# A feed-forward layer with per-batch weights: another order of the first loads and of the small steps behind them

## The chip, the cores and the metric

The kernel runs on one core of a Trainium2 chip. The core has TensorE for matrix products, VectorE, ScalarE and GpSimd for elementwise work, SyncE (SP) which issues most transfers, and 16 DMA engines between HBM and its on-chip memory SBUF. TensorE writes to PSUM. The metric is the device time of one execution in microseconds (us); the median of several runs is given.

## The reference

```python
W = weights[condition]                         # (64, 64, 64) out of 16 weights of 64x64
h = einsum('bct,bcd->bdt', x, W)               # per batch; x is (64, 64, 1024)
q = unpack6(qweight)                           # (1024, 1024) integers 0..63
w = (q - zero_point) * weight_scale            # per output row
out = x + einsum('bsk,nk->bsn', h, w) + bias   # (64, 64, 1024)
```

Every batch picks one of 16 small weights by its condition (stage 1). The result is multiplied with a large weight that is stored in 6 bits (stage 2). The input is added at the end. All is float32.

## The kernel before, in words

Two batches make a pair p, which fills the 128 partitions: the first batch lies in partitions LO (0 to 63), the second in HI (64 to 127). There are 32 pairs; two pairs make a group g. A value is multiplied as a high and a low half of 16 bits, so that the products keep the accuracy of float32: `hh` and `hl` are the halves of the result of stage 1, `xa` holds both halves of x, and `tab` those of the small weights. To bring the values into the range of the 16-bit type, they are scaled by a power of two, which is taken from a bound on sums of magnitudes: magnitudes (line 269, or 408 and 410 for the first two pairs), one small product on TensorE that spreads the bound (273 or 418), and a few bit operations on VectorE (`powers`, lines 138 to 142). Stage 2 (line 514) is eight K tiles (kt) of two halves and two banks of 512 columns, 32 products for a pair.

All work is put in order by hand. Each engine executes its instructions in the order in which they are written, and waits with semaphores for the others. The first pairs, 0 and 1, go an early way that needs less preparation. Their stage 1 is done in float32 (`early_stage1`, line 430) with `wbd`, a block diagonal of the two weights of the pair. `wbd` is copied out of the loaded weights `w32` by GpSimd and ScalarE (`early_select`, lines 389 and 391). Pair 0 has its x in two halves. The bound of a pair of this kind is the product of the weights' largest magnitude (`early_weights`, lines 396 and 397) and x's largest or summed magnitude (`early_magnitudes`). `early_rows` (line 413) multiplies them; `early_bounds` (418) spreads them on TensorE; `early_scales` makes the scales of it, which `early_high` and `early_low` (438, 445) use to write `hh` and `hl`. `weights_largest` (line 170) takes the largest magnitude of each of the 16 weights; it serves the scales of `tab`, and stands on VectorE ahead of the steps for pair 0. `unpack` (153, 155) takes the 6-bit fields out of the packed words `qr`.

From pair 2 on, stage 1 (line 490) uses the halves in `xa` and the weights of the pair in `wst`. Group 1 (pairs 2 and 3) has its halves written by `stacked_high` on ScalarE (318) and `stacked_low` on VectorE (326). Each of these is done twice for a pair, for the two halves of the partitions. From group 2 on, the halves are moved by DMA (333 to 339). A loop `window(p)` carries pairs 3 to 31, and the change does not touch it.

The transfers go to two queues. SP issues nearly all, in the order of lines 90 to 104; ScalarE issues `cb`, the conditions, and two small loads into a tile `ahead` that nothing reads. Eight semaphores serve the transfers in turn: a transfer waits at its issue until the one before it on the same semaphore has landed.

The tail of the early part, in which pairs 0 to 3 overlap, is the written order of lines 579 to 707. Line 654 (bounds of pair 3's x) stands ahead of the products of pair 1 with tiles 4 to 6 (line 658).

Of the kernel before, what the change touches and what calls it, by code (L numbers as in the profile page):

```python
# [8 lines left out]
F32 = mybir.dt.float32  # L9
# [3 lines left out]
U16 = mybir.dt.uint16  # L13
AF = mybir.ActivationFunctionType
ALU = mybir.AluOpType
# [4 lines left out]
QUNIT = 2.0**-24  # L20
# [9 lines left out]
def adaln_ffn(ctx: ExitStack, tc: tile.TileContext, x, cond, cw, qw, ws, wz, bias, out):  # L30
    nc = tc.nc
    B, C, T = x.shape
    _, NK, D = cw.shape
    N = qw.shape[2]
    P = 128
    NP = B // 2
    NG = NP // 2
    KT = T // P
# [6 lines left out]
    const = ctx.enter_context(tc.tile_pool(name="const", bufs=1))  # L45
# [15 lines left out]
    def load_pair(p, ts_=slice(0, T)):  # L61
        g, i = divmod(p, 2)
        if g not in xts:
            xts[g] = xp.tile([P, 2, T], F32, name="xt")
        nc.sync.dma_start(xts[g][:, i, ts_], xf[:, p, ts_])  # L65
# [10 lines left out]
    def load_q(w, n=1):  # L76
        nc.sync.dma_start(qr[:, w : w + n, :], qv[:, w // 2, w % 2 : w % 2 + n, :])

    w32 = const.tile([P, NK, D], F32, name="w32")
    cb = const.tile([NK, B], I32, name="cb")  # L80
# [3 lines left out]
    bib = const.tile([P, N], F32, name="bib")  # L84
    nc.scalar.dma_start(cb, cond.partition_broadcast(NK))

    ahead = const.tile([NK, 2, 16], F32, name="ahead")
    nc.scalar.dma_start(ahead[:, 0, :], x[0:4, 0 : C : C // 4, 0:16].rearrange("b c t -> (b c) t"))
    nc.scalar.dma_start(ahead[:, 1, :].bitcast(U16), qw[0, 0 : 2 * P : P // 8, 0:32])
    nc.sync.dma_start(w32[LO], cw[LO])  # L90
    load_pair(0, slice(0, T // 2))
    load_pair(0, slice(T // 2, T))
    load_pair(1)
    load_q(0)
    load_q(1)
    load_q(2, 2)
# [31 lines left out]
    kio = const.tile([NK, 1], F32, name="kio")  # L128
# [36 lines left out]
    hot = const.tile([P, B], BF, name="hot")  # L165
# [3 lines left out]
    def weights_largest():  # L169
        nc.vector.tensor_reduce(wmx[LO, 0:NK], w32[LO], AX.X, ALU.max, apply_absolute_value=True)  # L170
# [18 lines left out]
    def weights_powers():  # L189

        powers(tmp["pw"], tmp["pw"], wdn)

    def weights_scaled():
        nc.gpsimd.tensor_tensor(wsc, w32, wdn.unsqueeze(2).to_broadcast([P, NK, D]), ALU.mult)  # L194
# [6 lines left out]

    def weights_hot():

        nc.vector.tensor_scalar(hot[0:NK, :], cb, kio[:, 0:1], None, ALU.is_equal)

    def weights_own():

# [21 lines left out]
    def conditions_of(p, eng=nc.sync):  # L229
        conditions[p] = [  # L230
            eng.value_load(cb[0:1, 2 * p + j : 2 * p + j + 1], min_val=0, max_val=NK - 1) for j in range(2)
        ]
# [19 lines left out]
    st = {}  # L252
# [18 lines left out]
    def bounds(g, sl=BOTH):  # L271
        pl = ps_s.tile([P, 2], F32, name="pl", tag="s")
        nc.tensor.matmul(pl[:, sl], lhsT=ones, rhs=st[g]["l1"][:, sl], start=True, stop=True)  # L273
        st[g]["pl"] = pl
# [39 lines left out]
    def stacked_high(g, i):  # L314

        s = slice(i, i + 1)
        for j, (h, _) in enumerate(HALVES_OF):
            nc.scalar.activation(
                st[g]["xa"][h, i, j], xts[g][h, i], AF.Copy, scale=st[g]["down"][h, s], accum_out=st[g]["xs"][h, s]
            )  # L320

    def stacked_low(g, i, j):

        h, o = HALVES_OF[j]
        xa = st[g]["xa"]
        nc.vector.scalar_tensor_tensor(
            xa[o, i, j], xts[g][h, i], st[g]["down"][h, i : i + 1], xa[h, i, j], ALU.mult, ALU.subtract
        )
# [52 lines left out]
    updown = const.tile([P, 2, 2, 2], F32, name="updown")  # L381

    def early_select(p, j, eng):

        h = (LO, HI)[j]
        k = eng.value_load(cb[0:1, 2 * p + j : 2 * p + j + 1], min_val=0, max_val=NK - 1)
        to, of_ = wbd[h, p, h], w32[LO, ds(k, 1), :].rearrange("p o d -> p (o d)")
        if eng is nc.scalar:
            eng.copy(to, of_)
        else:  # L390
            eng.tensor_copy(to, of_)

    def early_weights(p):

        wl = const.tile([P, 1], F32, name=f"wl{p}")
        nc.vector.tensor_reduce(wl, wbd[:, p, :], AX.X, ALU.max, apply_absolute_value=True)
        nc.vector.tensor_scalar(wm[:, p, :], half, wl[:, 0:1], None, ALU.mult)
# [5 lines left out]
    def early_magnitudes(p, n, ts_, eng):  # L403

        xm[p, n] = const.tile([P, 1], F32, name=f"xm{p}{n}")
        if eng is nc.scalar:
            junk = ap.tile([P, T], BF, name="junk", bufs=1)
            nc.scalar.activation(junk[:, ts_], xts[0][:, p, ts_], AF.Abs, accum_out=xm[p, n])
        else:
            nc.vector.tensor_reduce(xm[p, n], xts[0][:, p, ts_], AX.X, ALU.max, apply_absolute_value=True)  # L410

    def early_rows(p, n):
        nc.vector.tensor_scalar(pb[:, p, n, :], wm[:, p, :], xm[p, n][:, 0:1], LEAST, ALU.mult, ALU.max)
# [7 lines left out]
    def early_scales(p):  # L421
        powers(tmp["pl"], updown[:, p, 0, :], updown[:, p, 1, :], least=False)

    def early_unscales(p):
        for j, h in enumerate((LO, HI)):
            nc.vector.tensor_scalar(st[0]["u"][h, p : p + 1], updown[h, p, 0, j : j + 1], 0.5 / QUNIT, None, ALU.mult)

    def early_stage1(p, ph, kts=range(KT)):
        for kt in kts:
            nc.tensor.matmul(  # L430
                ph[:, kt % ph.shape[1], :, :], lhsT=xts[0][:, p, ts(kt, P)], rhs=wbd[:, p, :], start=True, stop=True
            )

    def early_high(p, ph, kts):
        if p not in hs_pair:
            hs_pair[p] = [hp.tile([P, KT, P], F16, name="hh"), hp.tile([P, KT, P], F16, name="hl")]
        for j, h in enumerate((LO, HI)):
            nc.scalar.activation(
                hs_pair[p][0][:, kts, h], ph[:, :, j, :], AF.Copy, scale=updown[:, p, 1, j : j + 1]
            )  # L440
# [8 lines left out]
    def early_feature_sums(p):  # L449
        s = slice(p, p + 1)  # L450
        pu = ps_s.tile([P, 1], F32, name="pu", tag="s")
        nc.tensor.matmul(pu, lhsT=wbd[:, p, :], rhs=st[0]["xs"][:, s], start=True, stop=True)  # L452
        nc.vector.tensor_copy(st[0]["hs"][:, s], pu)
# [30 lines left out]
    def stage1(p):  # L484
        g, i = divmod(p, 2)
        ph = ps_o[0].tile([P, KT, 2, D], F32, name="ph")
        for kt in range(KT):
            for j in range(2):
                for a in range(2):
                    nc.tensor.matmul(  # L490
                        ph[:, kt, j, :],
                        lhsT=st[g]["xa"][:, i, j, ts(kt, P)],
                        rhs=wsts[g][:, i, a, j, :],
                        start=(a == 0),
                        stop=(a == 1),
                    )
        return ph.rearrange("p k j d -> p k (j d)")
# [26 lines left out]
    def stage2_tiles(p, kts, ks=range(2)):  # L524
        if p not in pos:
            pos[p] = ps_o[1 + p % 2].tile([P, N], F32, name="po", tag="po")
        products(pos[p], p, kts, ks, BANKS, BANKS)
# [49 lines left out]
    ph0a, ph0b = [ps_e.tile([P, KT // 2, 2, D], F32, name="ph0") for _ in range(2)]  # L577
# [2 lines left out]
    early_select(0, 1, nc.scalar)  # L580
    early_select(1, 0, nc.gpsimd)
    early_select(1, 1, nc.gpsimd)
    for n in range(2, 8):
        conditions_of(n, nc.gpsimd)
    weights_largest()
    early_weights(0)
    early_magnitudes(0, 0, slice(0, T // 2), nc.scalar)
    early_stage1(0, ph0a, range(0, 4))
    early_rows(0, 0)
    early_magnitudes(0, 1, slice(T // 2, 3 * T // 4), nc.vector)  # L590
    early_magnitudes(0, 2, slice(3 * T // 4, T), nc.scalar)
    early_rows(0, 1)
    early_rows(0, 2)
    early_weights(1)
    early_stage1(0, ph0b, range(4, KT))
    early_bounds(0, 3)
    early_scales(0)
    early_high(0, ph0a, LOWER)
    early_high(0, ph0b, UPPER)
    early_stage1(1, ph1)  # L600
    unpack(0)
    unpack(1)
# [5 lines left out]
    early_rows(1, 0)  # L608
    weights_turn()
    weights_diagonal()  # L610
    weights_hot()
    unpack(4, 2)
    stage2_tiles(0, range(0, 2), [1])
    unpack(6, 2)
# [3 lines left out]
    weights_bounds()  # L618
    early_bounds(1, 1)
    early_scales(1)  # L620
    weights_powers()
    weights_scaled()
    weights_own()
# [6 lines left out]
    early.close()  # L630
    ps_o.append(ctx.enter_context(tc.tile_pool(name="ps_b", bufs=1, space=bass.MemoryType.PSUM)))
    stacked_high(1, 0)
    for j in range(2):
        stacked_low(1, 0, j)
    weights_high()
    stage2_tiles(0, range(6, KT))
    early_feature_sums(0)
    early_feature_sums(1)
    magnitudes(1, 1)
    early_zero_points(0)  # L640
    early_unscales(0)
    weights_up()
    weights_low()
    unpacking.close()
# [6 lines left out]

    stage2_tiles(1, range(0, 4), [0])
    stage2_tiles(1, range(0, 4), [1])
    bounds(1, SECOND)
    scales(1, SECOND)
    early_minus(0)
    early_res(0)
    stage2_tiles(1, range(4, 7))
    stacked_high(1, 1)
    stacked_low(1, 1, 0)  # L660
    ph = stage1(2)
    stage1_high(2, ph, LOWER)
    stage1_high(2, ph, UPPER)
# [2 lines left out]
    magnitudes(2, 0)  # L666
    magnitudes(2, 1)
    stage1_low(2, ph)
    stacked_low(1, 1, 1)
    weights_of_batches()  # L670
    unscales(1)
    early_unscales(1)


    sums_high(1)
# [103 lines left out]
    p = NP - 1  # L779
# [67 lines left out]
```

## Time and profile before

| | |
|---|---|
| median of 3 runs | 266.77 us (266.57 to 267.13) |
| the profiled execution, its own time | 267.71 us |
| its span | 265.9 us |
| TensorE busy | 260.1 us (98%) |
| VectorE, ScalarE, GpSimd busy | 202.2, 161.7, 175.1 us |
| DMA moved | 53.34 MB, mean 201 GB/s |
| granted TensorE clock | 1.00 |

The profile shows one execution. Its span runs from the first to the last instruction; the execution's own time is longer by what lies around them. In a row of the timeline the first number is the start and the second the duration, both in us, then engine, line and operation, output and inputs, and in brackets how long the engine had been idle and what ended it. A row may hold several instructions (xN). PEld is TensorE's loading of weights, which overlaps the products. The chain that ended last is followed back from the last instruction, at each step to what released it.

### The profile page before, as it was taken

The page shows a single profiled execution, that of the slowest core. Times are in us where ns is not written, and L with a number is a line of the kernel's source. Part 1 is how long each engine was busy: PE and PEld are TensorE (multiplying, and loading weights), DVE is VectorE, ACT ScalarE, POOL GpSimd, SP SyncE. Part 2 cuts the span into 40 slices and gives each one's busy share as a digit, 9 for nine tenths or more (in the row PEclk, how much of TensorE's full clock was granted, in tenths as well). Part 3 has the DMA queues.
Part 4 walks back from the last instruction along what each step waited for, and adds up shares of the span by engine and source line. Part 5 has one row for each costly group of instructions (what it writes and reads, how often), then busy time and mean ns, then how long its engine had stood idle before and what let it go on. Part 6 is the DMA issues. An engine that isn't in the chain of part 4 may idle for free.

```text
span 265.9 us, 5725 instructions
## 1 busy us (share of the span) xinstructions
PE 260.1 (98%) x2159; PEld 139.9 (53%) x2159; DVE 202.2 (76%) x270; ACT 161.7 (61%) x289; POOL 175.1 (66%) x102
## 2 busy tenths in 40 slices
PE   7999999999999999999999999999999999999994
PEld 6655555555455555455555445555545555545553
DVE  3889999695977959598695968959597794955544
ACT  3799899665866556686555767556586555634100
POOL 4026457969595995959789595986829296595200
PEclk9999999999999999999999999999999999999999
DMA  6996078759649796589767797677976664551203
GB/s 178 327 368 239 2 168 261 217 168 270 199 106 325 195 293 178 168 245 238 260 181 225 240 264 244 156 243 217 291 220 178 218 160 137 163 160 79 83 35 123
DMA packets 31948, 53.34 MB, mean 201 GB/s; under 512 B 15152, under 2 KB 15408, under 8 KB 31920
## 3 DMA queue, kind: packets, MB, share of 16 engines
q1 hardware_dynamic: 31824, 52.96, 65.4%
q8 instruction: 17, 0.28, 0.4%
q14 instruction: 11, 0.09, 0.1%
q10 hardware_dynamic: 96, 0.01, 0.0%
HBM read 19.93 MB, written 16.78 MB: 138 GB/s over the span
## 4 chain that ended last, share of the span: by engine, by line
PE 95%; DMA 2%; SPq 1%; DVE 0%; issue 0%
PE po L514 81%; PE ph L490 11%; PE pe L514 3%; DMA xt<-in_x_dram 2%; PE ph L430 1%; PE pu L361 1%; SPq L65 0%; SPq L90 0%; DVE pe L555 0%; DVE xt L560 0%; PE pu L452 0%; PE pl L273 0%; PE pt L174 0%; PE pb__631 L220 0%; PE pl L418 0%
## 5 line engine op out<-in xcount | busy, mean ns | idle before, releaser
L514 PE MATMUL po<-q,hl 128*128 128x512 f16 x496 | 118.3, 379 | 0.0
L514 PE MATMUL po<-q,hh 128*128 128x512 f16 x496 | 118.3, 379 | 0.0
L550 POOL TENSOR_TENSOR xt<-xt,zt 128x1024 f32<-128x1024 f32 x28 | 79.0, 2839 | 48.4 <-ACT zt L548 48.4
L514 PEld LDWEIGHTS <-hl 128*128 128x128 f16 x520 | 50.6, 98 | 59.6 <-DVE hl L506 0.4
L502 ACT CAST hh<-ph 128x1024 f16<-128x1024 f32 (+1 forms) x31 | 30.4, 983 | 79.1 <-PE ph L490 41.5
L543 POOL TENSOR_TENSOR xt<-xt,bib 128x1024 f32<-128x1024 f32 x32 | 74.5, 2351 | 2.1 <-issue 2.1
L514 PEld LDWEIGHTS <-hh 128*128 128x128 f16 x520 | 48.4, 98 | 51.9
L555 DVE SCALAR_TENSOR_TENSOR po<-po,u,scb 128x1024 f32<-128x1024 f32 x27 | 34.8, 1287 | 49.2 <-PE po L514 49.2
L303 DVE SCALAR_TENSOR_TENSOR lf<-xt,down,hf 128x1024 f16<-128x1024 f32 x28 | 60.1, 2184 | 0.0
L506 DVE TENSOR_TENSOR hl<-ph,hh 128x1024 f16<-128x1024 f32 x30 | 36.5, 1216 | 0.1
L490 PEld LDWEIGHTS <-xa 128*128 128x128 f16 x960 | 32.1, 98 | 7.1
L560 DVE TENSOR_TENSOR xt<-po,xt 128x1024 f32<-128x1024 f32 x27 | 33.1, 1225 | 1.9
L490 PE MATMUL ph<-wst,xa 128*128 128x64 f16 x960 | 32.9, 193 | 0.0
L269 ACT ACTIVATE junk<-xt 128x1024 bf16<-128x1024 f32 x30 | 31.7, 1056 | 1.1 <-DMA xt<-in_x_dram 0.3
L293 ACT ACTIVATE hf<-xt,down 128x1024 f16<-128x1024 f32 x28 | 31.9, 1143 | 0.2 <-DVE down L139 0.2
L548 ACT ACTIVATE zt<-zsc,hs 128x1024 f32<-128x1024 f32 x28 | 30.5, 1138 | 0.0
L354 ACT ACTIVATE xh<-xh,xs 64x1 f16<-64x1 f16 x52 | 12.4, 287 | 0.5
L479 POOL TENSOR_TENSOR xt<-xt,res 128x1024 f32<-128x1024 f32 x4 | 9.5, 2365 | 0.0
L245 POOL COPY wst<-tab 128x128 f16 x12 | 4.9, 458 | 4.8 <-DVE tab L200 4.8
L194 POOL TENSOR_TENSOR wsc<-w,wdn 128x1024 f32<-128x1024 f32 x1 | 1.9, 1903 | 9.3 <-DMA w<-in_L_cond_weights_dram 9.3
L514 PE MATMUL pe<-q,hh 128*128 128x256 f16 (+1 forms) x24 | 6.6, 308 | 0.0
L514 PE MATMUL pe<-q,hl 128*128 128x256 f16 (+1 forms) x24 | 6.5, 308 | 0.0
(90 smaller groups left out, 121.3 us busy)
## 6 DMA issues: line engine op xcount, KB each, us to landing
out_dram<-xt SPq DMA_DIRECT2D x31, 512.0 KB, 3.0
xt<-in_x_dram SPq DMA_DIRECT2D x14, 1024.0 KB, 7.5
xa<-hf SPq DMA_DIRECT2D x24, 256.0 KB, 3.8
xa<-lf SPq DMA_DIRECT2D x24, 256.0 KB, 3.8
xt<-in_x_dram SPq DMA_DIRECT2D x3, 512.0 KB, 8.9
wst<-tab SPq DMA_DIRECT2D x48, 32.0 KB, 3.1
xa<-hf SPq DMA_DIRECT2D x8, 128.0 KB, 2.3
xa<-lf SPq DMA_DIRECT2D x8, 128.0 KB, 2.4
```

The lines of the kernel that those rows point to most:

```text
L269: nc.scalar.activation(junk, xts[g][:, i, :], AF.Abs, accum_out=st[g]["l1"][:, i : i + 1])
L293: nc.scalar.activation(st[g]["hf"][:, i, ts_], xts[g][:, i, ts_], AF.Copy, scale=st[g]["down"][:, i : i + 1], accum_out=st[g]["xs"][:, i : ...
L303: nc.vector.scalar_tensor_tensor(st[g]["lf"][:, i, ts_], xts[g][:, i, ts_], st[g]["down"][:, i : i + 1], st[g]["hf"][:, i, ts_], ALU.mult, ...
L490: nc.tensor.matmul(ph[:, kt, j, :], lhsT=st[g]["xa"][:, i, j, ts(kt, P)], rhs=wsts[g][:, i, a, j, :], start=(a == 0), stop=(a == 1),)
L502: nc.scalar.copy(hs_pair[p][0][:, kts, :], ph[:, kts, :])
L506: nc.vector.tensor_tensor(hl[:, kts, :], ph[:, kts, :], hh[:, kts, :], ALU.subtract)
L514: nc.tensor.matmul(po[:, a], lhsT=hs_pair[p][k][:, kt, :], rhs=qT[:, kt, c], start=(kt == 0 and k == 0), stop=(kt == KT - 1 and k == 1),)
L543: nc.gpsimd.tensor_tensor(xt, xt, bib, ALU.add)
L548: nc.scalar.activation(zt, zsc, AF.Copy, scale=st[g]["hs"][:, i : i + 1])
L550: nc.gpsimd.tensor_tensor(xt, xt, zt, ALU.subtract)
L555: nc.vector.scalar_tensor_tensor(po, po, st[g]["u"][:, i : i + 1], scb[:, cols], ALU.mult, ALU.mult)
L560: nc.vector.tensor_tensor(xts[g][:, i, cols], po, xts[g][:, i, cols], ALU.add)
```

## The change

Loads: the first half of pair 0's x is issued ahead of the weights, the second half behind them. Pair 1's x is issued as two halves. Of the two small loads on ScalarE's queue, the ones from x and from the packed words are gone, and one from the weights is there.

Small steps: `weights_hot` and `early_unscales` run on GpSimd, and stand earlier. The magnitude of the first half of pair 0's x runs on VectorE, ahead of `weights_largest`. The step `early_weights(1)` goes behind pair 0's scales.

Order up to pair 3: the feature sums of pairs 0 and 1 go ahead of pair 2's low halves; the bounds of pair 3's x go behind the products of pair 1 with tile 4; pair 3's second low half follows its first.

On TensorE the list of instructions is the same but for the place of one product, that of line 273 for pair 3. VectorE has three rows of instructions fewer in the listing, GpSimd the steps that left it.

```diff
-    ahead = const.tile([NK, 2, 16], F32, name="ahead")
-    nc.scalar.dma_start(ahead[:, 0, :], x[0:4, 0 : C : C // 4, 0:16].rearrange("b c t -> (b c) t"))
-    nc.scalar.dma_start(ahead[:, 1, :].bitcast(U16), qw[0, 0 : 2 * P : P // 8, 0:32])
+    ahead = const.tile([NK, 16], F32, name="ahead")
+    nc.scalar.dma_start(ahead, cw[0 : C : C // NK, 0, 0:16])
+    load_pair(0, slice(0, T // 2))
     nc.sync.dma_start(w32[LO], cw[LO])
-    load_pair(0, slice(0, T // 2))
     load_pair(0, slice(T // 2, T))
-    load_pair(1)
+    load_pair(1, slice(0, T // 2))
+    load_pair(1, slice(T // 2, T))
     load_q(0)
...
     def weights_hot():
-        nc.vector.tensor_scalar(hot[0:NK, :], cb, kio[:, 0:1], None, ALU.is_equal)
+        nc.gpsimd.tensor_scalar(hot[0:NK, :], cb, kio[:, 0:1], None, ALU.is_equal)
...
     def early_unscales(p):
         for j, h in enumerate((LO, HI)):
-            nc.vector.tensor_scalar(st[0]["u"][h, p : p + 1], updown[h, p, 0, j : j + 1], 0.5 / QUNIT, None, ALU.mult)
+            nc.gpsimd.tensor_scalar(st[0]["u"][h, p : p + 1], updown[h, p, 0, j : j + 1], 0.5 / QUNIT, None, ALU.mult)
...
     early_select(1, 1, nc.gpsimd)
+    weights_hot()
     for n in range(2, 8):
         conditions_of(n, nc.gpsimd)
+    early_magnitudes(0, 0, slice(0, T // 2), nc.vector)
     weights_largest()
+    early_stage1(0, ph0a, range(0, 4))
     early_weights(0)
-    early_magnitudes(0, 0, slice(0, T // 2), nc.scalar)
-    early_stage1(0, ph0a, range(0, 4))
     early_rows(0, 0)
...
-    early_weights(1)
     early_stage1(0, ph0b, range(4, KT))
     early_bounds(0, 3)
     early_scales(0)
+    early_unscales(0)
     early_high(0, ph0a, LOWER)
     early_high(0, ph0b, UPPER)
+    early_weights(1)
     early_stage1(1, ph1)
...
-    weights_hot()
...
     early_scales(1)
+    early_unscales(1)
...
     stacked_high(1, 0)
+    stage2_tiles(0, range(6, KT))
+    early_feature_sums(0)
+    early_feature_sums(1)
     for j in range(2):
         stacked_low(1, 0, j)
     weights_high()
-    stage2_tiles(0, range(6, KT))
-    early_feature_sums(0)
-    early_feature_sums(1)
     magnitudes(1, 1)
     early_zero_points(0)
-    early_unscales(0)
...
     stage2_tiles(1, range(0, 4), [1])
+    stage2_tiles(1, [4])
     bounds(1, SECOND)
     scales(1, SECOND)
     early_minus(0)
     early_res(0)
-    stage2_tiles(1, range(4, 7))
+    stage2_tiles(1, range(5, 7))
     stacked_high(1, 1)
     stacked_low(1, 1, 0)
+    stacked_low(1, 1, 1)
...
     stage1_low(2, ph)
-    stacked_low(1, 1, 1)
     weights_of_batches()
     unscales(1)
-    early_unscales(1)
```

## The prediction

> **What bounds the kernel now.** I read the page's busy times first, then the chain that ended last, then the timeline of the first 30 us with the waits of each engine, and last the landings of single tiles.
>
> ```profile
> PE 260.1 (98%) x2159; PEld 139.9 (53%) x2159; DVE 202.2 (76%) x270; ACT 161.7 (61%) x289; POOL 175.1 (66%) x102
> PE 95%; DMA 2%; SPq 1%; DVE 0%; issue 0%
> ```
>
> TensorE is busy 98% and carries 95% of the chain. So only what moves TensorE's start, or opens or closes a hole in it, can move the time. The chain in order of time shows where the start is decided:
>
> ```profile
> 2.48 5.83 DMA xt<-in_x_dram
> 8.31 0.14 issue
> 8.44 2.02 PE ph L430 x16
> 10.46 0.86 PE po L514 x4
> ...
> 25.73 3.45 PE po L514 x16
> 29.18 0.93 PE ph L490 x32
> ```
>
> Pair 1's x, issued at 2.48, lands at 8.31, and TensorE starts pair 1's first stage at 8.44. From there it never stops for long: 16 products of 512 columns take 3.45, 216 ns each. The waits of the PE rows after 8.44 add up to two holes, 0.11 at 30.0 (before line 361) and 0.09 at 35.4 (hl of pair 3). That is all that a better order can win there: 0.2 us.
>
> Before 8.44, and at the second place that matters, the timeline reads:
>
> ```profile
> 4.54 1.21 DVE L170 TENSOR_REDUCE wmx<-w 64x16 bf16<-64x1024 f32 x1 [1.45 <-DMA w<-in_L_cond_weights_dram]
> 5.67 0.27 DVE L396 TENSOR_REDUCE wl<-wbd 128x1 f32<-128x128 f32 x1
> 5.92 2.30 PE L430 MATMUL ph<-wbd,xt 128*128 128x128 f32 x16 [0.84 <-DMA xt<-in_x_dram]
> 7.04 0.42 DVE L410 TENSOR_REDUCE xm<-xt 128x1 f32<-128x256 f32 x1 [0.24 <-DMA xt<-in_x_dram]
> 7.49 0.38 DVE L413 TENSOR_SCALAR pb<-wm,xm 128x2 bf16<-128x2 f32 x2
> 8.05 0.22 PE L418 MATMUL pl<-pb,all_ones 128*128 128x2 bf16 x3
> 22.38 1.15 ACT L318 ACTIVATE xa<-xt,down 64x1024 f16<-64x1024 f32 x1 [0.53 <-DVE down L139]
> 24.91 1.07 ACT L502 CAST hh<-ph 128x512 f16<-128x512 f32 x2
> 25.54 3.14 PEld L514 LDWEIGHTS <-hh 128*128 128x128 f16 x16
> ```
>
> Landings: the weights at 4.43 (issued at 0.74, 3.7 to landing), the first x half at 5.78 (1.39 plus 4.4), the second at 7.01 (DVE's line 410 and PE's second half both start there). The three bound products (line 418) stand in TensorE's order ahead of pair 1. They end at 8.27, only 0.04 before x of pair 1. So two chains end together at 8.3: the loads, and VectorE's row of small steps behind the weights.
>
> **The Trainium skill.** "DMA: Bandwidth & Descriptors", "Issuing engines are not separate DMA queues": loads issued from SP and ACT run on the same 16 DMA engines and interleave. The trace agrees: the 1 KB load ahead of x takes 3.5 us to land, the 4 KB of cb, which meets nothing, 1.5. The same page's "Latency and other measured facts" says that most of a load's fixed cost of about 2 us is the round trip for the write's receipt. Here the 4 KB of cb take 1.5, and that part is paid in any place of the queue: a place earlier is worth only the data time of the load that is passed. "TensorE: Matmul & The Clock Gate", "Back-to-back issue gap", gives N/2.4 + 2.5 ns, 216 ns at 512 columns: what the chain shows, so nothing is left in the products themselves. "GPSIMD Engine Reference", 3.1, puts about 156 ns of dispatch on an instruction; this trace's small GpSimd steps take 0.11 (memset of 64x1) to 0.23 (copy of 64x64).
>
> **The change part by part.** Times against the profiled execution (span 265.9; own time 267.71, which is 0.94 over the median 266.77; I carry differences over to the median).
>
> *1. Order of the loads.* The weights go from first to second on SP, x's first half from second to first. The slots keep their sizes (256 KB each), so x's first half should land near 4.45 (0.74 plus 3.7). For the weights, W: at best little over the first slot's 4.43, since 16 KB per DMA engine must follow 16 KB, say 4.7; at worst the second slot's 5.8 of before. In that slot 15 of the 16 DMA engines had reported by 5.18 in the trace's semaphore records and one came 0.6 later; I take 5.3.
>
> VectorE's row behind W, by starts in the trace: 0.11 to start line 170; 1.13 to line 396; 0.31 to line 397; 0.27 to the first row (413); 0.26 to line 410; 0.45 to the last rows; 0.38 for both. Sum: rows ready at W + 2.91. (Before: W's line ended at 5.75, and from there x's halves set the pace, rows at 7.87.) Moving the first half's magnitude from ScalarE to VectorE costs about 0.68 there (line 170: 1024 elements in 1.21, 256 in 0.42), from 4.5 to 5.2, ahead of the weights. That is free while W is 5.07 or later, and caps the gain below. The last bound product then follows the rows by about 0.25 (0.07 of wait and 0.17 of product), so pair 1 starts at W + 3.16: with 5.3, at 8.46, +0.02 on 8.44. Break-even is W = 5.28, and each us later is a us lost. TensorE's own work on pair 0 starts at W + 0.35 (wbd is written 0.3 after W): 5.65, before the 5.92 of now, and no cost.
>
> *2. Pair 1's x in halves.* One SP issue more (0.43), and 2 KB packets for 4 KB ones, in the trace's DMA records 84 and 159 ns: 16 x 84 - 8 x 159 = 72 ns per engine. Half one lands by about 7.7, half two at 8.4, needed a microsecond into the stage. Gain: the wait for 8.31 goes, but the rows take its place. The loads behind: qr comes 0.07 later; line 155 for it may slip from 9.00 and 9.67 by 0.2, its first product is at 10.3. Cost 0. SP's waits move with the semaphores: zsb is issued after x's second half (about 7.1 instead of 6.36), pair 3's x about 0.7 later. The DMA engines are full from 6 to 20 us in stretches of 1 us (share 0.96 or more, but for one of 0.87), and zsb lands at 16.3 for a use at 20.71. Cost 0; with empty queues it would be 0.7 on a load with 4 us to spare.
>
> *3. The two small loads ahead.* x and qw are no longer touched ahead; cw is. Unknown: 0 to 0.5 us on x's or q's first packets, less 0.3 for a lighter start. I take 0. q's cover is about 0.5: hl of pair 0 (line 445) would end at 11.0, TensorE loads it at 11.16.
>
> *4. Steps to GpSimd.* hot (0.24) and four unscales (0.31 + 0.30) leave VectorE; GpSimd pays five instructions at 0.11 to 0.25, 0.6 to 1.2. It has nothing to do from 13.3, when its reads of the conditions end in the trace's records, to 15.42, where wsc waits for the second half of the weights; the reads start up to 0.9 later. wsc itself is read 1.4 after its end. Cost 0. line 396 for pair 1 goes behind pair 0's powers: 0.5 that VectorE spends before q at 9.3 instead of 8.3. Cost 0.
>
> *5. Second bounds of group 1 behind a tile.* Line 273 moves behind four products: from 21.12 to 21.98, ends at 22.15. From a bounds product's end to ScalarE's line 318 the first such pass took 0.46 (15.73 to 16.19), so line 318 starts at 22.61 instead of 22.38: +0.23. ScalarE is then solid until hh of pair 2 (24.91, first half 0.54, to 25.45), which TensorE loads at 25.54: a cover of 0.09. So 0.14 to 0.2 of new hole; bounds 0 to 0.25, I take 0.17. Queued behind it are all products of pair 2. The wait before line 361 at 30.0 moves with ScalarE: +0.05.
>
> *6. Low halves.* The sums' copies (0.21) come ahead of two low halves of 1.28 and wait for line 452, 0.3; the unscales that left pay for that. The last low half goes ahead of pair 2's hl: ready at 27.9 instead of 28.96 for a use at 29.0, hl at 29.2 for a use at 30.2. Both hidden. VectorE is 0.1 ahead at 34.2, while TensorE is 0.2 later: the 0.09 hole at 35.4 goes.
>
> Sum: +0.02 + 0.17 + 0.05 - 0.09 = +0.15 us; span 266.1, median 266.9.
>
> **Rivals.** *A, slower:* the weights land as late as the second load did, 5.8. Mechanism: line 170's 1.21 us start late, the rows (line 413) end at 8.71, pair 1 starts at 8.96: +0.52, and with the 0.13 of parts 5 and 6, +0.65: 267.4. It decides from W = 5.68. For it: that slot's measured landing. Against: only one engine was that late.
>
> *B, faster:* both first loads land early, x at 4.0 and the weights at 4.75, and x's second half by 6.7, where 10 of its 16 engines had reported by 5.5. Rows at 7.66, pair 1 at 7.91: -0.53; without the hole of part 5 and with the 0.2 of holes closed, -0.73: 266.0. For it: the late engines are few. Against: q would be the next thing late.
>
> *C, it does nothing:* the rows and x of pair 1 ended 0.04 apart before and do so again, and part 5's cover holds: 266.7.
>
> **Chances.** A 0.30, B 0.25, the forecast 0.30 and C 0.15. The smallest difference that a measurement of this kernel tells from none is about 0.2%, 0.53 us; the forecast and C lie inside, A and B outside. So faster 0.25, same 0.45, slower 0.30. The likeliest case alone spans 266.5 to 267.2; with A and B and the unknown of part 3 (0.5 on top of A's lower end), 266.0 to 267.7 leaves out about 2 in 10.
>
> **What would show it.** Right: line 170 starts near 5.4 and the rows end near 8.2; pair 1's first product at 8.3 to 8.6 waits for the bounds, not for x; ScalarE's first line 318 after 22 at about 22.6 plus the shift, and a hole of 0.1 to 0.2 in TensorE at 25.6; none at 35.4. Wrong: line 170 starts at 4.8 or after 5.8, pair 1 waits for x, or TensorE waits at 10.5 for q. A change of more than 1 us would mean a wait past 36 us, where I see no instruction moved.

## The result and the profile after

| | before | after |
|---|---|---|
| median of 20 runs each, on one chip | 267.14 us (266.57 to 267.69) | 267.63 us (267.40 to 268.16) |
| ratio of after to before | | 1.002, interval 1.0013 to 1.0027 |
| the profiled execution, its own time | 267.71 us | 267.60 us |
| its span | 265.9 us | 265.8 us |

The kernel became 0.49 us slower. The forecast was +0.15 on the median of 266.77 that it started from, rounded to 266.9. In the larger set of runs before itself has 267.14, so it is the differences that are compared here. Remarkable is what the two profiled executions say: after's is 0.11 *faster* than before's. So the pair of profiles can't explain the difference of the medians. The fastest of after's 20 runs, 267.40, is slower than before's median.

The page of after, its busy times and the shares of the chain that ended last:

```profile
PE 260.4 (98%) x2159; PEld 140.2 (53%) x2159; DVE 200.1 (75%) x266; ACT 161.1 (61%) x287; POOL 176.2 (66%) x107
PE 94%; DMA 2%; ACT 1%; DVE 1%; issue 1%; SPq 0%; DVEq 0%
```

TensorE still carries nearly all. New are the shares of ScalarE and VectorE, which the chain of after, in order of time, places:

```profile
1.19 4.09 DMA w<-in_L_cond_weights_dram
...
5.39 0.28 DVE wmx L170
...
7.67 0.24 DVE pb L413
...
8.25 1.96 PE ph L430 x16
...
22.36 1.25 ACT xa L318 x2
...
24.89 0.59 ACT hh L502
...
25.54 3.63 PE po L514 x16
```

Before's chain began with x of pair 1. Now it begins with the weights, which land at 5.28, and goes through VectorE's row of small steps to pair 1. A second detour, through ScalarE from 22.36 to 25.5, is also new. The timeline of after at the same places:

```profile
3.37 0.69 DVE L410 TENSOR_REDUCE xm<-xt 128x1 f32<-128x512 f32 x1 [0.27 <-DMA xt<-in_x_dram]
5.39 1.21 DVE L170 TENSOR_REDUCE wmx<-w 64x16 bf16<-64x1024 f32 x1 [1.33 <-DMA w<-in_L_cond_weights_dram]
7.67 0.36 DVE L413 TENSOR_SCALAR pb<-wm,xm 128x2 bf16<-128x2 f32 x2
7.96 0.29 PE L418 MATMUL pl<-pb,all_ones 128*128 128x2 bf16 x2 [0.22 <-DVE pb L413]
8.19 2.02 PE L430 MATMUL ph<-wbd,xt 128*128 128x128 f32 x16
21.73 0.17 PE L273 MATMUL pl<-l,ones 128*128 128x1 bf16 x1
25.53 3.14 PEld L514 LDWEIGHTS <-hh 128*128 128x128 f16 x16 [0.36 <-ACT hh L502]
35.39 1.89 PE L514 MATMUL po<-q,hl 128*128 128x512 f16 x8
```

TensorE waits for the bounds (0.22 before line 418), not for x, whose first half of pair 1 has been there since 6.53. It waits again at 25.5, for hh of pair 2: the first product with it starts 0.25 after the product ahead of it, instead of 0.03 as in before, a hole of 0.22. The hole at 35.4 is gone.

### The profile page after: what moved, and what is told of

The parts are those of the page before. It is cut to its first block, busy times and chain, and to the rows that moved or that the text cites. A ratio compares the mean times of both kernels' runs of the same rounds, so it can differ in the third digit from the quotient of the medians.

```text
span 265.8 us, 5724 instructions
## 1 busy us (share of the span) xinstructions
PE 260.4 (98%) x2159; PEld 140.2 (53%) x2159; DVE 200.1 (75%) x266; ACT 161.1 (61%) x287; POOL 176.2 (66%) x107
## 4 chain that ended last, share of the span: by engine, by line
PE 94%; DMA 2%; ACT 1%; DVE 1%; issue 1%; SPq 0%; DVEq 0%
PE po L514 80%; PE ph L490 10%; PE pe L514 3%; DMA w<-in_L_cond_weights_dram 2%; ACT xa L318 1%; PE ph L430 1%; PE pu L361 1%; ACT hh L502 0%; DVE pe L555 0%; DVE pb L413 0%; DVE xt L560 0%; SPq L65 0%; PE pu L452 0%; DVE xm L410 0%; PE pl L418 0%
## 5 line engine op out<-in xcount | busy, mean ns | idle before, releaser
L303 DVE SCALAR_TENSOR_TENSOR lf<-xt,down,hf 128x1024 f16<-128x1024 f32 x28 | 58.0, 2111 | 0.0
L344 ACT CAST xh<-xs 64x2 f16<-64x2 f32 x30 | 5.8, 193 | 0.4
```

What stands on the lines that cost most here:

```text
L303: nc.vector.scalar_tensor_tensor(st[g]["lf"][:, i, ts_], xts[g][:, i, ts_], st[g]["down"][:, i : i + 1], st[g]["hf"][:, i, ts_], ALU.mult, ...
```

## The experiments

The kernel "beside it" is before, measured together with the experiment on the same chip: its median is 267.29 for experiments 1 to 4, 267.19 for 5 to 8 and 267.25 for 9 to 12. After was not measured again beside them, so a difference to its 267.63 is one between two measurements. The ratio is not the quotient of the two medians; it differs from it by up to 0.15%, most in experiments 4 and 8, which have single runs far above the rest.

Two theories face each other at first. **S**: the profile of before shows a late start; its usual execution starts pair 1 earlier, and the new order of loads makes TensorE wait for VectorE's row every time. **P**: the profile of before is the usual execution, so its slack is what it shows. The first expectations set S against **H**: the start is the same, and the difference lies in what follows, around 25 us. What other letters stand for is said where they come.

**1. Before once more.** No edit.

> The kernel before, once more, for a second profile of it. Theory S (start): the first profile was a late draw. Its own time, 267.71, is 0.6 over the median of 20 runs, and five of the sixteen DMA engines brought pair 0's second half of x about 1.5 us late. A usual execution should start pair 1's first stage near 7.9 instead of 8.44, with pair 0's second half at about 6.0, and have a span near 265.3. Theory H (hole): the start is 8.4 again, and the difference to the changed kernel lies in what follows, around 25 us.

Measured: 267.30 against 267.29, ratio 0.9997 (0.9985 to 1.0008). Its single runs go from 266.63 to 267.78. But the execution whose trace was kept, the first of its 14 runs, is a late one again (267.68), as H said. In order of time, its chain has:

```profile
2.48 5.86 DMA xt<-in_x_dram
8.33 0.14 issue
8.47 2.02 PE ph L430 x16
```

So a second profile doesn't show S's early start; only the spread of the times speaks for it. Experiments 5 and 7 had to show it.

**2. The loads alone.** Before, with the diff's loads (order, halves, the load ahead) and the order of the first steps that belongs to them:

```diff
+    load_pair(0, slice(0, T // 2))
     nc.sync.dma_start(w32[LO], cw[LO])
-    load_pair(0, slice(0, T // 2))
...
+    early_magnitudes(0, 0, slice(0, T // 2), nc.vector)
     weights_largest()
-    early_weights(0)
-    early_magnitudes(0, 0, slice(0, T // 2), nc.scalar)
```

> Before, with the loads' part of the change alone: x's first half ahead of the weights, pair 1 in halves, one small load ahead, the first magnitude on VectorE. Theory S: pair 1 starts at 8.2 as in the changed kernel, since VectorE's row behind the weights (landing at 5.3) sets it; 0.3 us slower than before, ratio 1.001. Theory H: no difference to before beyond 0.1 us.

Measured: 267.62, ratio 1.0019 (1.0006 to 1.0031): +0.33 on the median beside it, with 3 of 22 runs at 269.1 to 269.4. In its trace the weights land at 5.82 and pair 1 starts at 8.73, behind the bounds:

```profile
5.93 1.21 DVE L170 TENSOR_REDUCE wmx<-w 64x16 bf16<-64x1024 f32 x1 [1.83 <-DMA w<-in_L_cond_weights_dram]
8.50 0.29 PE L418 MATMUL pl<-pb,all_ones 128*128 128x2 bf16 x2 [0.22 <-DVE pb L413]
8.73 2.02 PE L430 MATMUL ph<-wbd,xt 128*128 128x128 f32 x16
```

The loads make it slower without any of the other parts, and H, by which they make no difference, falls.

**3. The rest alone.** After, with the loads and the first steps of before (the reverse of 2):

```diff
-    load_pair(0, slice(0, T // 2))
     nc.sync.dma_start(w32[LO], cw[LO])
+    load_pair(0, slice(0, T // 2))
     load_pair(0, slice(T // 2, T))
-    load_pair(1, slice(0, T // 2))
-    load_pair(1, slice(T // 2, T))
+    load_pair(1)
```

> The complement: the small steps on GpSimd and the new order up to pair 3, with the loads and the first steps of before. Theory S: pair 1 starts as in before (7.9); the hole of 0.22 before pair 2's products is there, those at 30 and 35 are worth 0.1 less: together 0.1 to 0.2 slower than before. Theory H: 0.4 to 0.5 slower, the whole difference.

Measured: 267.49, ratio 1.0004 (0.9991 to 1.0018), +0.20 on the median beside it. The interval holds zero, so the times alone don't decide. Its trace has the hole before pair 2's products, of the same 0.22:

```profile
25.59 3.13 PEld L514 LDWEIGHTS <-hh 128*128 128x128 f16 x16 [0.36 <-ACT hh L502]
```

**4. Line 170 out of the row.** After, with `weights_largest` behind pair 0's powers:

```diff
-    weights_largest()
     early_stage1(0, ph0a, range(0, 4))
...
     early_unscales(0)
+    weights_largest()
```

> The changed kernel with the weights' largest magnitudes (line 170, 1.21 us on VectorE) behind pair 0's powers instead of ahead of its row of small steps. Theory S: the rows end 0.9 earlier, at 7.15; TensorE's own work on pair 0 then ends last, at 7.75, and pair 1 starts at 7.95 instead of 8.19: 0.25 us faster than the changed kernel, 0.25 slower than before. Theory H: no difference to the changed kernel.

A miss: 268.41, ratio 1.0052 (1.0031 to 1.0073), and 5 of 14 runs at 270.0 to 270.5. From its timeline:

```profile
6.32 3.70 PE L430 MATMUL ph<-wbd,xt 128*128 128x128 f32 x16 [0.81 <-POOL wbd L391]
12.34 1.02 PE L514 MATMUL po<-q,hh 128*128 128x512 f16 x4 [0.38 <-DVE q L155]
```

Two things came in. Pair 0's 16 products take 3.70 us instead of 2.02 (213 ns apart instead of 112): TensorE runs at its slow clock. And the 1.21 us of line 170, put back on VectorE at 10.30, push the unpacking behind it, so that TensorE waits for q. The step was moved to a place where it was no longer hidden.

**5 and 6. The row longer by a known amount.** Line 170 runs twice, in before and in after. This measures the slack of the row in the *times*, whatever one trace shows.

```diff
     weights_largest()
+    weights_largest()
```

> Before, with line 170 done twice: 1.21 us more on VectorE's row behind the weights. Theory S: in the usual execution of before pair 1 starts near 7.9, 0.4 to 0.5 behind what this row alone would allow (landing of the weights at 4.3, plus 3.16, 7.46); so 0.7 to 0.8 of the 1.21 come through, ratio 1.003. Rival P (the profile of before is the usual execution, start at 8.44 set by x): only 0.2 to 0.3 come through, ratio 1.001.

> The changed kernel with line 170 done twice. Theory S and rival P: the row sets the start, so all of the 1.21 comes through, 1.2 us over the changed kernel, 1.6 to 1.7 over before (ratio 1.006). If something else sets the start of the changed kernel (x, or TensorE's own work on pair 0), less comes through.

Before with it: 267.95 against 267.19 beside it, ratio 1.0028 (1.0021 to 1.0035), +0.76. Of the 1.21 us, 0.76 come through, so the row of before is usually only 0.45 us short of being the limit. By the profile of before it is 1.00 short: in the trace of experiment 7, where the row decides, pair 1 starts 3.01 after the weights land; before's landed at 4.43, which gives 7.44 against the 8.44 of its profile. P, by which about 0.2 come through, falls. After with it: 269.04 in six runs, ratio 1.0064 (1.0045 to 1.0083), +1.41 on after's median, though that was measured apart. Its trace shows it without that doubt: pair 1 starts 4.15 after the landing of the weights (5.45 to 9.60), in after 2.91, so all of the second pass comes through. After has no slack. From the timeline of before with the longer row:

```profile
4.62 2.46 DVE L170 TENSOR_REDUCE wmx<-w 64x16 bf16<-64x1024 f32 x2 [1.54 <-DMA w<-in_L_cond_weights_dram]
8.50 0.29 PE L418 MATMUL pl<-pb,all_ones 128*128 128x2 bf16 x2 [0.42 <-DVE pb L413]
8.73 2.02 PE L430 MATMUL ph<-wbd,xt 128*128 128x128 f32 x16
```

The wait before 8.50 is for the row. The times also close up (267.71 to 268.24): the landing of x, which spreads them in before, no longer decides.

**7. Weights first again.** After, with the weights first on SP, x's first half second, and the first steps in before's order; pair 1's halves and the single small load stay.

```diff
-    load_pair(0, slice(0, T // 2))
     nc.sync.dma_start(w32[LO], cw[LO])
+    load_pair(0, slice(0, T // 2))
```

> The changed kernel with the weights first on SP and x's first half second, and VectorE's and ScalarE's first steps in the order that goes with it; pair 1's x stays in halves, the single small load ahead stays. Theory S: as the kernel with the new order of steps alone, within 0.15 us (267.3 to 267.6), executions under 267.0 are there again. Rival L (the halves of pair 1 or the missing small loads ahead cost): it stays at 267.6, none under 267.3.

Measured: 267.16, ratio 0.9994 (0.9983 to 1.0005). The loss is gone, and the median lies even below S's range, though the hole of the other part should still cost; *Part 2* below comes back to it. Here the trace caught an early start; its timeline:

```profile
4.78 1.21 DVE L170 TENSOR_REDUCE wmx<-w 64x16 bf16<-64x1024 f32 x1 [1.70 <-DMA w<-in_L_cond_weights_dram]
7.17 0.36 DVE L413 TENSOR_SCALAR pb<-wm,xm 128x2 bf16<-128x2 f32 x2
7.68 2.02 PE L430 MATMUL ph<-wbd,xt 128*128 128x128 f32 x16
25.02 3.13 PEld L514 LDWEIGHTS <-hh 128*128 128x128 f16 x16 [0.36 <-ACT hh L502]
```

Weights at 4.67, row ended at 7.53, pair 1 at 7.68; the hole of the other part is still there. The order of the first steps went back with the weights, but it isn't what cost: from the landing to the end of the row it takes 2.86 here and 2.75 in after.

**8. Line 170 behind the rows.** After, with `weights_largest` behind `early_rows(0, 2)`, a shorter move than in 4:

```diff
-    weights_largest()
     early_stage1(0, ph0a, range(0, 4))
...
     early_rows(0, 2)
+    weights_largest()
     early_stage1(0, ph0b, range(4, KT))
```

> The changed kernel with line 170 behind the rows of pair 0 (line 413) and ahead of its powers, where VectorE waits for TensorE anyway. Theory S: rows at 7.1, pair 1 starts at 7.95 behind TensorE's own work on pair 0 instead of 8.19; VectorE's later steps start where they did (8.3). So 0.1 to 0.25 faster than the changed kernel, if hl of pair 0 comes in time for it (cover under 0.1); rival P the same. If it is not faster, VectorE's steps behind the powers have taken over.

Measured: 267.47, ratio 1.0025 (1.001 to 1.004). In its trace line 170 no longer stands ahead, and pair 1 starts 0.40 earlier than in after:

```profile
7.79 2.03 PE L430 MATMUL ph<-wbd,xt 128*128 128x128 f32 x16
```

The median is only 0.16 lower, with 4 of 22 runs at 269.2 to 270.0, and the ratio to before isn't lower than after's 1.002: the times don't show a gain. The row was the limit in the trace; with it shorter, TensorE's own products for pair 0 decide, and they too hang on the weights' late landing.

**9. Line 273 back.** After, with the bounds of pair 3 ahead of tile 4, as in before:

```diff
-    stage2_tiles(1, [4])
     bounds(1, SECOND)
...
-    stage2_tiles(1, range(5, 7))
+    stage2_tiles(1, range(4, 7))
```

> The changed kernel with line 273 for pair 3's x back ahead of tile 4 of pair 1; all else stays. If part 5 of the prediction holds, ScalarE's line 318 starts 0.2 earlier against TensorE, the hole of 0.22 before pair 2's products closes, and the time falls by 0.15 to 0.22: about 267.45. Rival: the hole is taken up later anyway, no difference.

A miss in the median: 267.82, ratio 1.0024 (1.0011 to 1.0037). Its trace has no hole at hh of pair 2, but the weights landed at 6.39 and pair 1 started at 9.30:

```profile
6.50 1.21 DVE L170 TENSOR_REDUCE wmx<-w 64x16 bf16<-64x1024 f32 x1 [2.49 <-DMA w<-in_L_cond_weights_dram]
26.42 3.62 PE L514 MATMUL po<-q,hh 128*128 128x512 f16 x16
```

Which of the two the median shows could not be told from it alone; the next kernel takes the landing out.

**10. Weights first, and line 273 back.** Both edits, 7 and 9:

```diff
-    load_pair(0, slice(0, T // 2))
     nc.sync.dma_start(w32[LO], cw[LO])
+    load_pair(0, slice(0, T // 2))
...
-    stage2_tiles(1, [4])
     bounds(1, SECOND)
...
-    stage2_tiles(1, range(5, 7))
+    stage2_tiles(1, range(4, 7))
```

> The kernel with the weights first and the new order of steps, with line 273 back as well: 0.15 to 0.2 under the 267.16 of the former, 267.0, which would be 0.2 under before (ratio 0.999). Rival: 267.15.

Measured: 266.84 against 267.25, ratio 0.9991 (0.9983 to 1.0): the fastest of all, at the edge of what can be told from no change, and 0.32 below experiment 7. In its timeline pair 1 starts at 7.55, and ScalarE is ahead of TensorE at pair 2:

```profile
21.47 1.15 ACT L318 ACTIVATE xa<-xt,down 64x1024 f16<-64x1024 f32 x1 [0.51 <-DVE down L139]
24.00 1.07 ACT L502 CAST hh<-ph 128x512 f16<-128x512 f32 x2
24.68 3.62 PE L514 MATMUL po<-q,hh 128*128 128x512 f16 x16
```

The first half of hh is there at about 24.54, and the products start at 24.68 without a wait.

**11. More work ahead.** Theory C holds that the runs at 269 to 270 come from TensorE standing idle between its dummy products and pair 0, so that its clock is not full; six more dummy products would cover it. The kernel of experiment 8 with:

```diff
-    WARM = 40
+    WARM = 46
```

> The kernel with line 170 behind the rows, with 46 instead of 40 products on dummy data at the start. Theory C (clock): the executions of that kernel at 269 to 270, 4 of 22, are those in which TensorE stands still for 0.65 us behind the dummy products and runs the float32 products at 213 ns apart instead of 129, as the first execution of the kernel with line 170 behind the powers did. With the gap filled, none is over 268.3, and the median stays within 0.15 of 267.47. Rival: they have another cause, and 1 in 6 is still there.

A miss: 267.77, ratio 1.0018 (1.0004 to 1.0032); two of 21 runs still at 269.8 and 269.9, three more above 268.3. Its trace is one of them, and shows that the weights were so late, 6.41, that six more products did not reach to them:

```profile
6.84 3.75 PE L430 MATMUL ph<-wbd,xt 128*128 128x128 f32 x16 [0.69 <-POOL wbd L391]
```

Idleness alone isn't the cause either. In the trace of experiment 9 TensorE was idle longer, and its products ran at full speed:

```profile
6.82 2.02 PE L430 MATMUL ph<-wbd,xt 128*128 128x128 f32 x16 [1.62 <-POOL wbd L391]
```

There the clock had been full since 4.75, ahead of the idleness, as the dummy products show (106 ns apart until then, 56 after); here, and in experiment 4, it had not. That fits C in a narrower form, an idle stretch *before* the clock is full, but two traces are no proof. The last section has what all fourteen traces say of it.

**12. The small load alone.** Theory A holds that the single small load ahead, from the weights instead of from x and the packed words, is what brings x earlier in 7. Before, with that edit alone:

```diff
-    nc.scalar.dma_start(ahead[:, 0, :], x[0:4, 0 : C : C // 4, 0:16].rearrange("b c t -> (b c) t"))
-    nc.scalar.dma_start(ahead[:, 1, :].bitcast(U16), qw[0, 0 : 2 * P : P // 8, 0:32])
+    nc.scalar.dma_start(ahead, cw[0 : C : C // NK, 0, 0:16])
```

> Before, with only the small loads ahead changed: one from the weights in the place of the two from x and from the packed words. Theory A: those two delay single DMA engines; without them pair 0's second half of x lands by 6.3 instead of near 7.0, pair 1 starts near 7.7 and the median falls by 0.2 to 0.3, to 266.9 to 267.0. Rival (the halves of pair 1, not the loads ahead, brought x earlier in the kernel with the weights first): no difference to before.

Measured: 267.18, ratio 1.0003 (0.9991 to 1.0014). No gain in time. Pair 1 starts at 8.13 in its trace, behind its undivided x (8.00).

**All traces in one table.** Behind pair 1's first product TensorE hardly stops. So an execution's own time less that start should be a constant, plus any hole that a kernel has behind it. It is, and it sorts the kernels by their order of steps behind the start:

| order of before | start, us | own time less start |
|---|---|---|
| before | 8.44 | 259.27 |
| before once more (1) | 8.47 | 259.21 |
| loads alone (2) | 8.73 | 259.19 |
| row longer, before (5) | 8.73 | 259.24 |
| small load alone (12) | 8.13 | 259.28 |

| order of after, line 273 back | start, us | own time less start |
|---|---|---|
| line 273 back (9) | 9.30 | 259.14 |
| both back (10) | 7.55 | 259.15 |

| order of after, line 273 behind tile 4 | start, us | own time less start |
|---|---|---|
| after | 8.19 | 259.41 |
| the rest alone (3) | 8.26 | 259.38 |
| row longer, after (6) | 9.60 | 259.40 |
| weights first (7) | 7.68 | 259.41 |
| line 170 behind the rows (8) | 7.79 | 259.50 |
| more work ahead (11) | 10.51 | 259.41 |
| line 170 late (4), which has the wait for q | 9.93 | 260.20 |

Without the last three rows, which also move line 170, the means are 259.24, 259.15 and 259.40. So the place of line 273 costs 0.25 us, the rest of the new order wins 0.09, and the part behind the start costs 0.16 in all. If the constant holds for the runs without a trace too, the median time gives the usual start: before 267.14 - 259.24 = 7.90, after 267.63 - 259.40 = 8.23. So of the +0.49, 0.33 is a later start and 0.16 what follows; single traces of one order differ by up to 0.09, so these are good to some 0.05. After's profile (8.19) is a usual execution of its kernel, before's (8.44) one of its latest.

## Why the prediction came out as it did

The median lies in the predicted range, 0.07 below its upper end, and on the side of rival A. The difference is 0.34 above the forecast's own (+0.49 against +0.15). That the range held is in part luck: the forecast's own case, 266.5 to 267.2, did not.

*Part 1, the loads: mechanism right, the size wrong; this is the term that was mis-sized.* Taken for the weights: 5.3; measured 5.28. The rows were to end at W + 2.91; they ended at 8.03, W + 2.75, since line 410 followed its row by 0.13 instead of 0.26. The start followed them by 0.16 instead of 0.25. So pair 1 started 0.27 earlier than the forecast's 8.46. But it was compared with 8.44, and the usual start of before is 7.90. "I carry differences over to the median" was the wrong sentence: the profiled execution was noted to be 0.94 over the median, and that excess sat in the very stage that the change touches. With the usual start in its place, the forecast's own 8.46 would have meant +0.56, and the measured start means +0.33. Two errors, 0.54 (8.44 for 7.90) and 0.23 (8.46 for 8.23), partly cancelled.

Why weights in the second place cost time at all is that x's landing could be hidden and theirs can't. In the seven traces with the weights first they land at 4.22 to 4.67; in the seven with them second, at 5.28 to 6.41. VectorE's row of some 2.75 us hangs on them. x's first half lands at 3.35 when it is first (4.45 was predicted: a slot was taken to have one landing time for 256 KB, but in the first one x took 2.6 us from its issue and the weights 3.5 to 3.9), and then nothing can be done with it for two us but one magnitude. In times: of 121 runs of the six kernels with the weights second and the row not lengthened, none is under 267.0 us and 17 are over 269; of 77 runs of the five changed or repeated kernels with the weights first, 27 are under 267.0 and none is over 269. (Of 187 runs of before beside all of these, 46 and one.)

*Part 2, halves:* they landed at 6.53 and 8.22 (7.7 and 8.4 predicted); nothing waits for them. The cost of nothing was right for after. What was not seen is that they may be worth something once the weights are first: by the constants of the table, the usual start is 7.76 in experiment 7 and 7.69 in 10, against 7.95 and 8.01 of before beside them. The halves are what sets these two apart from before in the loads, besides the small load that did nothing alone; on their own they were not run.

*Part 3, the small loads:* no effect was taken, and none was found (experiment 12). TensorE doesn't wait for q at 10.5.

*Part 4, steps to GpSimd:* hidden, as said, but not at the sizes given. hot takes 0.48 and the four unscales 1.03 together, 1.51 against the estimated 0.6 to 1.2. In all VectorE has 266 instructions for 270, GpSimd 107 for 102. wsc behind them starts at 15.38, as before at 15.42.

*Part 5, line 273:* right. ScalarE's line 318 starts 0.46 after the bounds' product ends (21.90 to 22.36), the very distance that was used, and the hole is 0.22 for 0.17. The wait before line 361 hardly grew, 0.01 for 0.05.

*Part 6:* right, the hole at 35.4 is gone. The three terms were to sum to 0.13 (0.22 for line 273 less 0.09); the table says 0.16 (0.25 less 0.09).

*Rivals.* A had the direction, the chain and nearly the size (+0.65), but not the landing: it needed the weights at 5.8, and was said to decide only from 5.68. They came at 5.28 in after's trace, as the forecast took them. With the usual start, every landing behind 4.99 (7.90 less the 2.91 from landing to start) costs time. B (faster) needed the weights at 4.75, which no trace with them second shows. C (nothing) failed on the hole and on the start alike.

*What stays open.* What makes one landing later than another was not found; it differs between measurements as well: experiment 9 shares after's first 20 us of instructions, and its usual start by the table is 8.67 against 8.23. A late landing comes from a part of the 16 DMA engines: in experiment 9's trace eleven had reported the weights by 5.07, the other five at 5.75 to 6.39. In 7 and 10 the second half of pair 0's x lands at 5.74 and 5.87, in the four unlengthened kernels with pair 1's x whole at 6.4 to 7.1; whether the halves do that was not run alone. And the trigger of the slow clock is read from the traces (last section); no run tested it.

## What to carry to other kernels

Before you subtract from a profiled time, ask whether that execution is a usual one. If its own time is off the median, find which stage holds the excess; when it is the stage that you change, the slack that the profile shows isn't the slack that you have, and lengthening the suspected chain by a known amount measures the real one. In this kernel the first place in the queue belongs to the load with the longest chain of dependent steps behind it, not the one whose consumer is named first.

## What the runs showed of the hardware

Where a transfer lands varies far more than what an engine takes: the same 256 KB of weights, second in the queue, landed 4.1 to 5.2 us after their issue at 1.19, while one execution of line 170 took 1.20 to 1.21 in every trace.

TensorE's float32 products of stage 1 are 112 ns apart at the full clock and 213 ns at the slow one (by their starts in the traces; the 129 in the expectation of experiment 11 is too much), and the clock became full between 3.90 and 10.51 us after the span's start, although every kernel but one ran the same 40 dummy products from 1.06. The Trainium skill ("TensorE: Matmul & The Clock Gate", Part 1, on the clock gate) says that the clock becomes full after about 3.4 us of sustained work, by a window that runs freely, so that the number of slow products differs from run to run. The traces agree that it differs, and they show the window, a fixed stretch of time: in each of the fourteen, the record of the full clock lasts 256.00, 259.41 or 262.83 us, lengths that differ by about 3.41.

In twelve traces the clock became full between 3.90 and 6.80. The two late ones, 9.82 in experiment 4 and 10.51 in experiment 11, are one window behind 6.41 and 7.10, and in the window that ended there TensorE was idle for 0.81 and 0.69 us ahead of pair 0. Of the windows that did make the clock full, the one with most idle time had 0.57 (experiment 10, ahead of the dummy products). So by these traces 0.69 us of idle time in the deciding window costs one window more at the slow clock, while 1.62 us after the clock had become full, in experiment 9, cost nothing. This was worked out from the traces afterwards, and no run tested it.

That slow products cost up to 1.7 us at a start (3.70 and 3.75 against 2.02 for 16) shows when they stand on the path; in before's second profile six of them were slow and hidden behind the wait for x. The mean granted clock in the page read 1.00 in those traces and doesn't show it.
